# Early expert tiles: products up on two pairs of PSUM banks, and the next tile's transposes ahead of a tile's product down

## The chip, the cores and the metric

The kernel runs on one core of a Trainium2 chip. The metric is the device time of one execution in microseconds (us). The core has a tensor engine (PE, with its weight loads shown as PEld), a vector engine (DVE), a scalar engine (ACT), GpSimd (POOL) and a sync engine (SP), which here issues nearly all DMAs and does no arithmetic. Everything is in 32-bit floats. A matmul writes into PSUM; the program holds PSUM as eight banks of 128 partitions by 512 floats, and other engines read the results from there.

## The reference

The input x has shape (2, 2048, 256). Four sub-layers follow one another, each added to x, each on a layer norm of x:

```
x = x + ssm(layernorm(x))         # Mamba-2 block, 8 heads of 64, state 128, conv of 4
x = x + ffn(layernorm(x))         # mixture of experts
x = x + attention(layernorm(x))   # 16 heads of 64, softmax over the two entries of the batch
x = x + ffn(layernorm(x))         # the same mixture of experts again
```

The mixture of experts has 8 experts; a token takes the two with the highest scores:

```
idx = top_k(scores + bias, 2);  val = softmax(scores)[idx], divided by its sum
h = x @ Wl1[n] + bl1[n]                          # 256 -> 2 x 512, halves a and b
y = (silu(a) * b) @ Wl2[n] + bl2[n]              # 512 -> 256
out = sum over the token's two experts of val * y
```

The kernel computes only the products of the chosen experts. It sorts tokens by expert into tiles of up to 256 tokens.

## The kernel before

**A tile of an expert.** The class `Experts` exists twice, for the first feed-forward (`ffn`, names with `_f`) and for the last (`last`, names with `_g`). `load` (L663) issues on SP the expert's weights w1 (1 MB) and w2 (0.5 MB) and the biases b1 and b2; `rows` (L652) loads the tile's list of tokens and gates, tab; `gather` (L680) fetches the tokens' rows xs by an indirect DMA on POOL, 128 rows each. `turn` (L702) transposes xs on PE (4 matmuls against the identity, into a bank called pxs), and ACT copies the result to xT. `up_part` (L716) makes a quarter of the product up: 4 matmuls into one bank pab (the trace counts each of them as two, so 32 for a tile), then silu of the one half on ACT (sa) and the gate product on DVE (gT). `down` (L745) has 8 matmuls (16 in the trace) into a bank pf, ACT and DVE scale the result by the gate (by, y), and POOL adds y to the output in memory by two indirect DMAs.

**Early tiles.** Tokens are routed while the SSM (or, for `last`, the attention) is still going over later positions. As soon as an expert has 256 tokens from the part that is done, a tile can be computed. The dictionaries EARLY say how many such tiles there are after which group: 21 for `ffn` (names `_fe`, during the SSM), 9 for `last` (`_ge`, at the end of the attention). The rest is done by `run` (L814), where no other work stands between tiles.

The generator `early` (L790) makes the instructions of the early tiles. It yields after each half of the product up and after the product down, and the loop over the SSM's chunks (32 chunks of 128 positions, in 8 groups of 4) takes three steps of it per chunk: about one early tile per chunk. `fetch` loads two tiles ahead. Weights, xs and xT of early tiles have two buffers each, gT one.

**PSUM.** There is one pool of four tags, T, A, B and C, with two banks each, and the tags go round: the third tile of a tag waits until the first has been read. Early tiles use tag B for everything (pxs, pab, pf), and B is also used by the SSM for pb, pd and pe and by the routing. Tag A is used by the SSM for pc (the input of the conv, L990) and pz (the gate, L1037). Late tiles, in `run`, take A and B in turn for pab and T for pxs.

**The SSM's chunk.** `chunk_front` makes pz, then the decay factors lt: eight ACT instructions (L1044) on lb, which is a broadcast of the running sums over all partitions. `spread` (L1021) issues that DMA on SP two chunks ahead, into one of two buffers. Then follow exp (with a load of ACT's function table), px and pb. `chunk_back` has py, ph and pi, `chunk_out` the transposes pty and the product po.

**What sets the order.** SP's queue is in the order of the program's text; all loads stand there, and an SP instruction that waits for a buffer holds all behind it. Within a chunk SP has w1, w2, b1, b2 of the next tile and then lb. The order on PE, DVE, ACT and POOL outside `run` is set by a planner from costs and dependences, not by the text, so a change in banks can move instructions there.

Of the kernel before, what the change touches and what calls it, by code (L numbers as in the profile page):

```python
# [46 lines left out]
def kernel(  # L47
# [232 lines left out]
    class Experts:  # L280
# [509 lines left out]
        def early(self, ready):  # L790

            i = 0
            while True:
                while i >= len(self.seq):
                    yield
                if not self.seq[i][4]:
                    return
                full = sum(t[4] > 0 for t in self.seq)
                self.fetch(min(i + 2, full), min(i + 2, full))
                self.fetch(full, 0)  # L800
                if not i:
                    yield
                self.turn(i)
                t = self.ts[i]
                t["gT"] = fe.tile([P, NHT, TT], F32, tag="gT", name=f"gT_{t['nm']}", bufs=1)
                for j in range(NHT):
                    self.up_part(t, j, "B")
                    if j % 2:
                        yield
                self.down(i, "B", None)  # L810
                i += 1
                yield
# [45 lines left out]
    with tc.tile_pool(name="ssm1", bufs=1) as s1, tc.tile_pool(name="ssm2", bufs=2) as s2:  # L858
# [315 lines left out]
        for i, (b, s, t) in enumerate(chunks):  # L1174
            j = order.index((b, s)) + 1
# [365 lines left out]
```

## Time and profile before

| | us |
|---|---|
| three runs: median (lowest to highest) | 1698.82 (1694.02 to 1705.58) |
| the profiled execution | 1695.92 |
| its span | 1694.1 |

The mean granted clock of the tensor engine is 0.972 of full speed. The stages, read from the names of the instructions in the timeline, with PE's busy time in them:

| stage | window, us | PE busy, us |
|---|---|---|
| SSM, no early tiles yet | 0 to 300 | 255.3 |
| SSM with early tiles of the first feed-forward | 300 to 670 | 346.3 of 370 |
| the rest of the early tiles, alone | 670 to 740 | 63.6 of 70 |
| first feed-forward, `run` | 740 to 880 | 137.4 of 140 |
| attention | 896 to 1250 | 342.1 of 354 |
| attention's end, with the first early tiles of the last feed-forward | 1250 to 1315 | 62.5 of 65 |
| the rest of these early tiles, alone | 1315 to 1405 | 83.3 of 90 |
| last feed-forward, `run` | 1405 to 1640 | 235.0 of 235 |

In the profile's groups an arrow points from inputs to output ("pab_fe<-xT_fe,w_fe"), followed by shapes, counts, busy time in us, the mean in ns and the idle time ahead of them. In timelines and chains each row starts with its start in us and its length; brackets give the idle time before it and what ended it.

### The profile page before, as it was taken

How to read it: one execution, taken by the hardware profiler on the slowest of the kernel's cores; microseconds unless marked ns; L12 is line 12 of the kernel's file. 1: busy time of each engine (PE TensorE's matmuls, PEld its weight loads, DVE VectorE, ACT ScalarE, POOL GpSimd, SP SyncE). 2: the span in 40 equal slices, each digit the busy share in tenths (PEclk: the TensorE clock that was granted, in tenths of full speed). 3: DMA queues.
4: the chain of work that ended last, by engine and by line, in shares of the span. 5: the costliest groups of instructions: out<-in, count | busy, mean ns of one | idle time of the engine just before them, and what ended most of it. 6: DMA issues, size and time to landing. Idle time of an engine off the chain costs nothing.

```text
span 1694.1 us, 22151 instructions
## 1 busy us (share of the span) xinstructions
PE 1584.1 (94%) x7088; PEld 1193.8 (70%) x7088; DVE 897.0 (53%) x2471; ACT 670.9 (40%) x1338; POOL 736.2 (43%) x702
## 2 busy tenths in 40 slices
PE   6997988989989989999998999899999999999997
PEld 4664555677766777788885566475767878888886
DVE  6778878837648464422226757547554622222222
ACT  4886867856647543222332201101020322333322
POOL 2356357455555566634442002422240663544443
PEclk9898988999989999999999999999999999999999
DMA  4112202742535455889852231706435588888883
GB/s 157 38 54 60 88 28 61 215 126 61 168 63 160 125 144 131 209 244 320 230 133 82 54 72 52 100 13 139 144 62 150 147 215 240 222 231 229 230 215 48
DMA packets 174744, 231.30 MB, mean 137 GB/s; under 512 B 45920, under 2 KB 138080, under 8 KB 174368
## 3 DMA queue, kind: packets, MB, share of 16 engines
q1 hardware_dynamic: 143520, 193.42, 38.9%
q0 software_dynamic: 31104, 36.42, 12.0%
q8 instruction: 58, 0.95, 0.2%
q14 instruction: 62, 0.51, 0.1%
HBM read 192.72 MB, written 37.06 MB: 136 GB/s over the span
## 4 chain that ended last, share of the span: by engine, by line
PE 66%; DVE 12%; DMA 11%; POOL 5%; ACT 3%; issue 3%; SPq 1%; DVEq 0%; POOLq 0%; ACTq 0%
PE pab_g L722 9%; PE pao L1431 7%; PE pab_fe L722 5%; PE pq L1337 5%; PE pab_f L722 5%; PE pf_g L754 4%; PE pf_fe L754 4%; PE pab_ge L722 3%; DVE xc L1007 3%; PE pk L1337 3%; PE pvd L1411 3%; PE pi L1103 2%; DMA lb<-sums 2%; PE pc L990 2%; PE pf_f L754 2%
## 5 line engine op out<-in xcount | busy, mean ns | idle before, releaser
L722 PE MATMUL pab_g<-xT_g,w_g 128*128 128x256 f32 (+1 forms) x896 | 181.6, 361 | 0.0
L722 PE MATMUL pab_fe<-xT_fe,w_fe 128*128 128x256 f32 x672 | 157.8, 390 | 20.0 <-DVE gT_fe L731 17.1
L722 PEld LDWEIGHTS pab_g<-xT_g,w_g 128*128 128x128 f32 x896 | 158.5, 191 | 19.4 <-ACT xT_g L713 0.4
L722 PEld LDWEIGHTS pab_fe<-xT_fe,w_fe 128*128 128x128 f32 x672 | 128.5, 194 | 46.9 <-DVE gT_fe L731 21.8
L778 POOL DMA_INDIRECT out_dram<-y_g,tab_g x51 | 80.3, 1575 | 137.4 <-DVE y_g L767 57.9
L730 ACT ACTIVATE sa_g<-pab_g,b_g 128x256 f32<-128x256 f32 (+1 forms) x112 | 50.9, 454 | 191.3 <-PE pab_g L722 191.3
L731 DVE SCALAR_TENSOR_TENSOR gT_g<-pab_g,b_g,sa_g 128x256 f32<-128x256 f32 (+1 forms) x112 | 51.5, 460 | 129.0 <-ACT sa_g L730 129.0
L1337 PE MATMUL pq<-w_qkv_sb,axT 128*128 128x512 f32 x256 | 117.1, 597 | 0.0
L1007 DVE SCALAR_TENSOR_TENSOR xc<-pre,conv_w_sb,xc 128x512 f32<-128x512 f32 x144 | 113.3, 796 | 6.0 <-ACT xc L999 5.4
L1431 PE MATMUL pao<-w_o_sb,o 128*128 128x256 f32 x512 | 112.3, 380 | 0.0
L1431 PEld LDWEIGHTS pao<-w_o_sb,o 128*128 128x128 f32 x512 | 97.1, 190 | 15.8 <-issue 2.6
L433 POOL DMA_INDIRECT table_g<-pay_g,at_g x64 | 62.7, 980 | 86.2 <-DVE w_g L409 52.7
L990 PE MATMUL pc<-xT,w_in_sb 128*128 128x512 f32 x192 | 97.4, 638 | 0.4 <-ACT xc L999 0.4
L722 PE MATMUL pab_f<-xT_f,w_f 128*128 128x256 f32 (+1 forms) x512 | 96.6, 347 | 0.0
L754 PE MATMUL pf_g<-w_g,gT_g 128*128 128x256 f32 x408 | 92.9, 380 | 0.0
L722 PEld LDWEIGHTS pab_f<-xT_f,w_f 128*128 128x128 f32 x512 | 85.5, 191 | 9.4
L1044 ACT ACTIVATE lt<-lb,cum 128x128 f32<-128x128 f32 x256 | 82.8, 394 | 19.0 <-DMA lb<-sums 19.0
L1337 PEld LDWEIGHTS pq<-w_qkv_sb,axT 128*128 128x128 f32 x256 | 48.6, 192 | 58.8 <-issue 57.4
L1352 ACT ACTIVATE kd<-pk 128x512 f32<-128x512 f32 x32 | 19.1, 597 | 162.4 <-PE pk L1337 96.0
L778 POOL DMA_INDIRECT resid<-y_fe,tab_fe x42 | 67.0, 1595 | 37.5 <-DVE y_fe L767 21.9
L731 DVE SCALAR_TENSOR_TENSOR gT_fe<-pab_fe,b_fe,sa_fe 128x256 f32<-128x256 f32 x84 | 39.7, 480 | 80.5 <-ACT sa_fe L730 80.4
L754 PE MATMUL pf_fe<-w_fe,gT_fe 128*128 128x256 f32 x336 | 80.3, 392 | 2.2 <-DVE gT_fe L731 2.2
(477 smaller groups left out, 3368.6 us busy)
## 6 DMA issues: line engine op xcount, KB each, us to landing
w_g<-in_wl_dram SPq DMA_DIRECT2D x28, 1024.0 KB
w_fe<-in_wl_dram SPq DMA_DIRECT2D x21, 1024.0 KB
lb<-sums SPq DMA_DIRECT2D x32, 512.0 KB
w_f<-in_wl_dram SPq DMA_DIRECT2D x16, 1024.0 KB
o<-prob SPq DMA_DIRECT2D x32, 512.0 KB
w_g<-in_wl_dram SPq DMA_DIRECT2D x28, 512.0 KB
w_fe<-in_wl_dram SPq DMA_DIRECT2D x21, 512.0 KB
w_ge<-in_wl_dram SPq DMA_DIRECT2D x9, 1024.0 KB
```

The source lines that it names most:

```text
L433: i = nc.gpsimd.indirect_dma_start(out=self.table, out_offset=bass.IndirectOffsetOnAxis(ap=at[:, t, c : c + 1], axis=0), in_=pay[:, t, c, ...
L722: nc.tensor.matmul(p[:, q * n : (q + 1) * n], t["w1"][:, k, c * P : (c + 1) * P], t["xT"][:, k, :], start=(k == 0), stop=(k == KD - 1),)
L730: nc.scalar.activation(sa[:, :n], p[:, 0:n], AF.Silu, bias=t["b1"][:, i : i + 1])
L731: nc.vector.scalar_tensor_tensor(t["gT"][:, i, :n], p[:, n : 2 * n], t["b1"][:, NHT + i : NHT + i + 1], sa[:, :n], ALU.add, ALU.mult)
L754: nc.tensor.matmul(pos[h][:, h * DM : (h + 1) * DM], t["gT"][:, j, h * P : (h + 1) * P], t["w2"][:, j, :], start=(j == 0), stop=(j == NHT ...
L778: j = nc.gpsimd.indirect_dma_start(out=self.acc if self.direct else self.acc[: self.seq[i][4] or NT + TT, :], out_offset=bass.IndirectOffs ...
L990: nc.tensor.matmul(pc, w_in_sb[:, k, DI + c * P : DI + (c + 1) * P], xT[:, k, :], start=(k == 0), stop=(k == KD - 1),)
L1007: nc.vector.scalar_tensor_tensor(xc[:, c, :], pre[:, c, j : j + TG], conv_w_sb[:, c, j : j + 1], xc[:, c, :], ALU.mult, ALU.add,)
L1044: nc.scalar.activation(lt[:, i, :], lb[:, i, :], AF.Relu, bias=g["cum"][:, t, i : i + 1], scale=-1.0)
L1337: nc.tensor.matmul(p, src[:, k, t * P : (t + 1) * P], w_qkv_sb[:, k, j, half * TG : (half + 1) * TG], start=(k == 0), stop=(k == KD - 1),)
L1411: nc.tensor.matmul(pvd, w_qkv_sb[:, k, 2, c * P : (c + 1) * P], xd[:, k, :], start=(k == 0), stop=(k == KD - 1),)
L1431: nc.tensor.matmul(po[:, j * DM : (j + 1) * DM], o[i][:, c, (t + j) * P : (t + j + 1) * P], w_o_sb[:, c, :], start=(c == 0), stop=(c == NA ...
```

## The change

In `early`, three things:

```diff
                 if not i:
                     yield
-                self.turn(i)
+                if "xT" not in self.ts[i]:
+                    self.turn(i)
                 t = self.ts[i]
                 t["gT"] = fe.tile([P, NHT, TT], F32, tag="gT", name=f"gT_{t['nm']}", bufs=1)
                 for j in range(NHT):
-                    self.up_part(t, j, "B")
+                    self.up_part(t, j, "AB"[j % 2])
                     if j % 2:
                         yield
+
+                if i + 1 in self.ts and self.seq[i + 1][4]:
+                    self.turn(i + 1)
                 self.down(i, "B", None)
```

The four quarters of an early tile's product up take tags A and B in turn, where all took B. Before a tile's product down, the next tile is turned (its transposes and the copy to xT) if it has been loaded and is an early one. A tile that has been turned in this way is not turned again. The transposes of early tiles still go to tag B.

## The prediction

> **What bounds the kernel now.** I read the page's busy totals and costliest groups first, then the waits of the tensor engine (PE), then the chain of waits inside the stretch where most of them fall, then the engines' timelines there.
>
> ```profile
> PE 1584.1 (94%) x7088; PEld 1193.8 (70%) x7088; DVE 897.0 (53%) x2471; ACT 670.9 (40%) x1338; POOL 736.2 (43%) x702
> ...
> L722 PE MATMUL pab_fe<-xT_fe,w_fe 128*128 128x256 f32 x672 | 157.8, 390 | 20.0 <-DVE gT_fe L731 17.1
> ```
>
> PE is the bound: 94% of the 1694.1 us span, so all its idle time is 110 us and no removal of waits can give more. An early tile's product up (pab_fe) costs 390 ns a matmul, that of the last stage (pab_g) 361 in the same page, and 17.1 us of idle stand before it.
>
> ```profile
> PE pab_fe L722 <- DVE gT_fe L731: 17.1, 13, 4.3
> ...
> PE pab_ge L722 <- ACT xT_ge L713: 3.1, 4, 1.1
> ...
> PE pab_fe L722 <- ACT xT_fe L713: 2.7, 4, 0.7
> PE pab_ge L722 <- DVE y_ge L767: 2.5, 1, 2.5
> ```
>
> Columns: total, times, longest. The first is the wait for a PSUM bank: a pab bank is free when its gate product gT has read it. The xT rows are waits for the copy behind a tile's transposes. Why the bank is late in the stage of the SSM with early tiles (300 to 670 us) is in the chain of waits there (start, length):
>
> ```profile
> 351.17 5.87 DMA lb<-sums
> ...
> 357.37 0.97 ACT lt L1044 x3
> 358.34 0.37 ACT sa_fe L730
> 358.73 0.49 DVE gT_fe L731
> 359.22 0.04 issue
> 359.27 3.72 PE pab_fe L722 x16
> ```
>
> and in ACT's timeline of the next chunk:
>
> ```profile
> 378.78 1.57 ACT L1044 ACTIVATE lt<-lb,cum 128x128 f32<-128x128 f32 x5 [2.89 <-DMA lb<-sums]
> 380.25 0.45 ACT L730 ACTIVATE sa_fe<-pab_fe,b_fe 128x256 f32<-128x256 f32 x1
> ```
>
> ACT is in order. The SSM's lt waits for its broadcast lb; the silu sa_1 of the tile stands behind it; gT_1 behind that; and pab_2 wants that bank. lb in turn is issued on SP behind the next weight load w2, which waits for an earlier product down (pf). So pf, SP, lb, ACT, gT, PE is a loop. PE then lies idle and afterwards runs slowly:
>
> ```profile
> 378.70:381.30 2.60, 0.06 (x2) 0.03 (x1) 0.56 (x2) 2.52 (x9) 0.00 (x0) 1.00 0.14 22
> 381.30:386.70 5.40, 5.40 (x18) 4.39 (x19) 2.99 (x5) 5.01 (x7) 2.85 (x2) 0.68 0.01 0
> ```
>
> (window, PE busy, PEld, DVE, ACT, POOL, granted clock, DMA share, GB/s.) Where early tiles run alone ("tails", 670 to 740 and 1315 to 1405 us) a tile is
>
> ```profile
> 1359.98 7.17 PE L722 MATMUL pab_ge<-xT_ge,w_ge 128*128 128x256 f32 x32 [0.67 <-ACT xT_ge L713]
> 1366.99 3.67 PE L754 MATMUL pf_ge<-w_ge,gT_ge 128*128 128x256 f32 x16
> 1370.50 0.60 PE L709 MATMUL pxs_ge<-ident,xs_ge 128*128 128x128 f32 x4
> 1371.77 7.17 PE L722 MATMUL pab_ge<-xT_ge,w_ge 128*128 128x256 f32 x32 [0.67 <-ACT xT_ge L713]
> ```
>
> 11.8 us a tile, 0.67 of it idle.
>
> **The change part by part.** No instruction, byte or DMA is added or removed: 30 tiles keep their 32 up matmuls, 4 transposes, 16 down matmuls, evictions and DMAs. SP's queue, which issues w1, w2, b1, b2, the tables and lb, keeps its order exactly, so nothing is moved past a load there. What changes is bank and order on PE, ACT, DVE and POOL; the order of the changed program shows where.
>
> *Banks.* pab_1 and pab_3 stay on B with pb, pxs and pf; pab_0 and pab_2 go to A, which the SSM uses for pz and pc. pab_2 now needs the A bank that pab_0 left, whose gT_0 is ready early, and in most chunks the planner puts sa_1 ahead of lt. So the wait before pab_2 goes. By place its 13 parts are 0.26, 1.32, 2.54, 0.25, 1.05, 1.74, 4.30, 0.31, 1.48, 1.70 and 0.98 in the mixed stage (15.9) and 0.31 and 0.85 in the tail.
>
> What is late next: pf needs gT_3, which stands behind sa_2 and sa_3, and those still stand behind lt, its exp and two table loads. From pf to pf the loop is 3.45 (pf, from the chain) + 1.8 (end of pf to start of lb: 1.6, 1.8 and 2.0 in three chunks) + 6.2 (lb: 5.9, 6.2, 6.6) + 8.3 (eight lt 2.5, sz .6, bt .25, table 1.28, exp 1.06, table 1.28, two silus .9, gT .5, as in the timeline) = 19.8 us. PE's own work in a plain chunk is 19.3 (20.62 less its stall of 1.32), and about 21.7 where the next group's transposes (.9) and dt projection (1.7) fall in. So a plain chunk comes to about 19.8 instead of 20.6 to 21.2: from pf start to pf start 20.62, 20.80, 20.94 and 21.17 before, gains .8, 1.0, 1.1 and 1.4; the chunk from 594.5 (22.16) about 1.5; sum 5.8.
>
> The two long stalls are worth more. *Row:* behind the 2.54 us stall the next 16 pab take 5.41 us against 3.72 and the following pf 5.00 against 3.67, clock 0.68, .94 and .73: with the matmuls between about 3.5 us. Behind the 4.30 us one it is 6.08 and 5.00, clock 0.60: 4.1 us. *Rule:* "TensorE: Matmul & The Clock Gate", Part 1, has the array drop to half clock after about 3.4 us without activity, counted in a free-running window. By it alone the 2.54 us stall costs no clock and its chunk gains 1.3; by the row it gains more. I take the row: chunk 366 to 393 goes from 26.5 to PE's 21.7 (4.8), chunk 470 to 499 from 28.9 to 22.3 (its lb took 8.76, which lengthens the loop by 2.5): 6.6. By the rule the sum of all would be 3.5 lower.
>
> Mixed stage so far 5.8 + 4.8 + 6.6 = 17.2. Given back: pxs_fe13 waits for its gather, whose routing table comes at a fixed time after its group, so 1.9 us gained just ahead of it are lost; and around the first early tile pc_2 to pc_5 of the next group move behind the tile, about 13 us later. They feed 12 conv steps on DVE (796 ns each on the page), for which px and pb then wait. No row shows that: 0 at one end, since the group's first chunk is still a tile away; 4 at the other (near the 4.1 us that PE's pt_m waits for one DVE step elsewhere in the waits); I take 2.5. Net 12.8.
>
> *The turn ahead.* The 4 transposes and the xT copy move ahead of pf. In a tail the copy (0.6) is hidden behind pf (3.5), and the next pab follows at once: 4 x 0.68 in the first tail, 1.10 + 3 x 0.67 in the second. With the bank waits and late gT rows there (.31, .85, .88) the first tail loses 4.8 of idle. In the second, pvd now stands behind tile ge1's products, so the 2.51 for y_ge goes, with .24, .47 and 1.25 for gates: 7.6, in all about 8.
>
> The turn is also a new wait. PE's matmuls run in program order ("TensorE: Matmul & The Clock Gate", Part 2, says that only weight loads are pulled ahead), so a transpose that waits for its gather holds a pf that is ready; this speaks against the change. In the trace gathers of early tiles land well before their turn but for three waits (1.05, 1.14, 1.61), so I price it where it shows. One transpose of the run stage's first tile (pxs_f0, pxs_g0) now stands ahead of pf of the last but one early tile. Its table is loaded behind a w2 that waits for a pf: the gather lands some 11.2 (f) and 11.9 us (g) after the end of the pf before, and is wanted 7.4 after. New stalls 3.8 and 4.5, in place of 1.6 and 1.7. By the rule of no reordering this is paid in full; if PE found other work it would be nothing. I take it in full: first tail 4.8 - 2.2 = 2.6, second 8.0 - 2.8 = 5.2.
>
> *Sum:* 12.8 + 2.6 + 5.2 = 20.6 us. The profiled execution takes 1695.9 (span 1694.1 and 1.8 around it), 2.9 under the median of the three runs, 1698.8. 1695.9 - 20.6 = 1675.3; at the median 1678.
>
> **The rivals.**
> *The wait only moves.* The loop binds with its whole length and the stall before pab_2 is found again before pf, clock loss too. For: the loop's 19.8 is above PE's 19.3, and DMA lb has 25% of the chain between 325 and 400 us. Against: sa_1 no longer stands in the loop, and only two chunks had stalls that cost clock. Then the tails alone count: 1698.8 - 7.8 = 1691.
>
> *Slower: turns hold PE.* Transposes ahead of pf wait for gathers in tile after tile, because the faster chunk asks for them sooner and POOL issues them between scatters of 1.6 us. Each such stall of 2.5 to 4.3 costs 3.5 to 4.1 of clock behind it, about 7. Three use up the 20.6; six make 42, so 1698.8 + 21 = 1720. For: the three gather waits above. Against: gathers stand ahead of the scatters on POOL in the changed order, and tables are fetched tiles ahead. The same price holds if A banks shared with pc and pz make the conv late at every group.
>
> *More.* All of the 15.9 us, the 7.6 of clock and 8 in the tails go: 1698.8 - 31 = 1668. It needs lb to land sooner than the loop lets it.
>
> **How the numbers follow.** About 1%, 17 us, is what a measurement of this kernel can tell from no change. Forecast 0.45, of it 0.08 short of 17 us; more 0.12; wait only moved 0.27; slower 0.16. Faster 0.49, same 0.35, slower 0.16. The range 1663 to 1706 takes in the first three cases and two or three stalls of the slower one.
>
> **What would show it.** Right: pab_fe <- gT_fe almost gone; a new pf_fe <- gT_fe of 3 to 8 us; pab waits on xT gone; tail tiles of 11.1 us; granted clock 0.9 and more at 381 to 398 and 486 to 504; new waits of pxs_f and pxs_g of about 4 us. Wrong: pf waits as long as the pab waits were, clock under 0.8 in the mixed stage, long waits of pxs_fe for xs_fe, or px and pb waiting for conv.

## The result and the profile after

The changed kernel took 1712.1 us in the median of 16 runs (1704.1 to 1721.1), the kernel before 1699.8 us beside it: a ratio of 1.0071 with a 95% interval of 1.0056 to 1.0087. It is slower by 12 us, where 1678 and a range of 1663 to 1706 had been forecast. The profiled execution has a span of 1710.2 us, 16.1 more than before.

The page of the changed kernel, its busy totals and the row of the product up of early tiles:

```profile
PE 1598.7 (93%) x7088; PEld 1210.3 (71%) x7088; DVE 901.8 (53%) x2471; ACT 667.5 (39%) x1334; POOL 733.5 (43%) x702
...
L722 PE MATMUL pab_fe<-xT_fe,w_fe 128*128 128x256 f32 x672 | 155.8, 385 | 3.8 <-ACT xT_fe L713 2.1
```

The wait that the change was about is gone: 3.8 us of idle before pab_fe and not 20.0. Yet PE's idle time is no smaller (1710.2 - 1598.7 = 111.5 us, before 110.0), and the same 7088 matmuls keep it busy for 14.6 us longer. Idle time has moved, and PE has run more slowly. PE's waits of the changed kernel say where to (total, times, longest, in us):

```profile
PE pi L1107 <- DVE y L1093: 7.8, 5, 2.6
PE pd L925 <- ACT xT L259: 7.0, 3, 4.0
...
PE pe L972 <- DVE da L965: 5.1, 2, 4.0
...
PE pf_fe L754 <- ACT xT_fe L713: 3.5, 2, 3.2
...
PE pab_fe L722 <- DVE gT_fe L731: 1.7, 2, 1.0
```

In the kernel before, the first three of these are smaller, there is no row of pf waiting for xT, and the last row has 17.1:

```profile
PE pi L1103 <- DVE y L1089: 4.0, 5, 1.6
...
PE pe L968 <- DVE da L961: 1.3, 2, 1.1
...
PE pd L921 <- ACT xT L259: 0.5, 1, 0.5
```

A good milestone is the start of pf of the 17th early tile (pf_fe16), where the stage of the SSM with early tiles is all but over: 688.2 us before, 703.2 after. So 15.0 of the 16.1 us are lost by then. In the windows that end there (window, PE busy, PEld, DVE, ACT, POOL, granted clock, DMA share, GB/s; the kernel before first)

```profile
285.00:688.20 403.20, 375.54 (x1738) 287.62 (x1738) 245.99 (x707) 225.35 (x443) 219.46 (x194) 0.96 0.48 131
285.00:703.20 418.20, 387.36 (x1734) 300.55 (x1734) 250.37 (x700) 221.29 (x439) 217.54 (x193) 0.92 0.46 126
```

PE is busy for 11.8 us longer and idle for 3.2 us longer (30.8 and 27.7), with a lower granted clock. So about four fifths of the loss is the same work done more slowly. From there to the attention it is 222.3 us (221.0 before), and the early tiles of the last feed-forward take 156.4 (156.9).

Two places show how the loss comes about. The first is the first early tile, in PE's timeline of the changed kernel:

```profile
304.60 0.66 PE L1132 MATMUL pty<-ident,y 128*128 128x128 f32 x4 [0.23 <-DVE x L1144]
309.23 0.41 PE L972 MATMUL pe<-da,tri 128*128 128x32 f32 x2 [3.98 <-DVE da L965]
...
313.75 6.76 PE L722 MATMUL pab_fe<-xT_fe,w_fe 128*128 128x256 f32 x16 [1.40 <-ACT xT_fe L713]
```

PE waits 3.98 us for da with nothing to do, then for the copy, and the next 16 pab take 6.76 us (3.62 where the clock is full). In the kernel before, pc_2 stood ahead of pe and pc_3 ahead of pab_0, and pe waited 0.17:

```profile
305.76 1.94 PE L990 MATMUL pc<-xT,w_in_sb 128*128 128x512 f32 x4
307.87 0.41 PE L968 MATMUL pe<-da,tri 128*128 128x32 f32 x2 [0.17 <-DVE da L961]
...
311.30 3.10 PE L990 MATMUL pc<-xT,w_in_sb 128*128 128x512 f32 x4
314.23 3.62 PE L722 MATMUL pab_fe<-xT_fe,w_fe 128*128 128x256 f32 x16
```

The second place is a chunk in which the next group begins:

```profile
388.00 1.02 PE L1100 MATMUL ph<-wx,bt 128*128 128x512 f32 x2
391.48 0.51 PE L925 MATMUL pd<-w_in_sb,xT 128*128 128x16 f32 x2 [2.46 <-ACT xT L259]
391.82 0.88 PE L709 MATMUL pxs_fe<-ident,xs_fe 128*128 128x128 f32 x3
392.50 3.01 PE L925 MATMUL pd<-w_in_sb,xT 128*128 128x16 f32 x14
395.34 3.65 PE L1107 MATMUL pi<-dtx,lt 128*128 128x64 f32 x16
398.79 0.42 PE L709 MATMUL pxs_fe<-ident,xs_fe 128*128 128x128 f32 x1
399.00 5.03 PE L754 MATMUL pf_fe<-w_fe,gT_fe 128*128 128x256 f32 x16
```

ACT's timeline shows why xT is late there:

```profile
383.34 1.57 ACT L1048 ACTIVATE lt<-lb,cum 128x128 f32<-128x128 f32 x5 [2.29 <-DMA lb<-sums]
...
390.11 0.84 ACT L730 ACTIVATE sa_fe<-pab_fe,b_fe 128x256 f32<-128x256 f32 x2
390.84 1.07 ACT L259 COPY xT<-pt_a 128x512 f32<-128x512 f32 x2
```

Between these rows stand the rest of lt, its exp and two loads of ACT's function table. It is the old chain, lb, lt, exp, silus, with another end. Where pab_2 waited 2.54 us before, pd now waits 2.46; where it waited 4.30, pd waits 4.03. Behind both stands half clock, in the windows of the changed kernel (the granted clock is the third number from the end):

```profile
391.50:399.00 7.50, 7.50 (x36) 7.50 (x37) 1.75 (x6) 1.93 (x3) 2.25 (x2) 0.51 0.02 2
499.40:513.50 14.10, 14.08 (x55) 12.32 (x56) 6.05 (x23) 3.27 (x6) 5.10 (x5) 0.59 0.00 0
```

### The profile page after: what moved, and what is told of

It reads as the page before. It is cut to its first block, busy times and chain, and to the rows that moved or that the text cites. A ratio compares the mean times of both kernels' runs of the same rounds, so it can differ in the third digit from the quotient of the medians.

```text
span 1710.2 us, 22153 instructions
## 1 busy us (share of the span) xinstructions
PE 1598.7 (93%) x7088; PEld 1210.3 (71%) x7088; DVE 901.8 (53%) x2471; ACT 667.5 (39%) x1334; POOL 733.5 (43%) x702
## 3 DMA queue, kind: packets, MB, share of 16 engines
q0 software_dynamic: 31104, 36.42, 11.8%
## 4 chain that ended last, share of the span: by engine, by line
PE 69%; DVE 11%; DMA 9%; POOL 5%; ACT 4%; issue 2%; SPq 1%; DVEq 0%; POOLq 0%; ACTq 0%
PE pab_g L722 9%; PE pao L1435 6%; PE pq L1341 6%; PE pab_fe L722 6%; PE pab_f L722 5%; PE pf_g L754 4%; PE pf_fe L754 4%; DVE xc L1011 3%; PE pk L1341 3%; PE pi L1107 3%; PE pab_ge L722 3%; DMA o<-prob 3%; PE pvd L1415 3%; PE pf_f L754 3%; PE pc L994 2%
## 5 line engine op out<-in xcount | busy, mean ns | idle before, releaser
L722 PEld LDWEIGHTS pab_g<-xT_g,w_g 128*128 128x128 f32 x896 | 158.3, 190 | 19.8 <-ACT xT_g L713 0.5
L754 PE MATMUL pf_fe<-w_fe,gT_fe 128*128 128x256 f32 x336 | 85.3, 412 | 4.8 <-ACT xT_fe L713 3.5
L1107 PEld LDWEIGHTS pi<-dtx,lt 128*128 128x128 f32 x512 | 71.2, 218 | 22.2 <-DVE y L1093 12.8
L1107 PE MATMUL pi<-dtx,lt 128*128 128x64 f32 x512 | 72.8, 301 | 11.0 <-DVE y L1093 7.8
```

Source lines behind the costliest of these rows:

```text
L722: nc.tensor.matmul(p[:, q * n : (q + 1) * n], t["w1"][:, k, c * P : (c + 1) * P], t["xT"][:, k, :], start=(k == 0), stop=(k == KD - 1),)
L754: nc.tensor.matmul(pos[h][:, h * DM : (h + 1) * DM], t["gT"][:, j, h * P : (h + 1) * P], t["w2"][:, j, :], start=(j == 0), stop=(j == NHT ...
L1107: nc.tensor.matmul(pi[:, i * HD : (i + 1) * HD], f["lt"][:, i, :], f["dtx"][:, i * HD : (i + 1) * HD], start=True, stop=True,)
```

## The experiments

All ratios are to the kernel before on the same chip in the same runs. The batches differed, on four chips: the kernel before took 1707 to 1731 us there, so times are not compared from one batch to the next. The changed kernel itself was measured on the first chip only. Profiles are used to see where a wait stands, ratios for its size; the start of a pf in the tables is that of one profiled execution (the row "before" is the first chip's; a second profile, before_again, has 344.6 and 690.5). That of first_b is the fastest of its 22 runs, 17 us under their median.

### One half of the change at a time, and two repairs

Three theories stood at first: that the wait only moves along the late ACT (1), that the turn ahead makes pf wait (2), and that sharing tag A reorders the SSM's work into DVE's way (3). Later ones are told in the expectations that they belong to.

banks_only and turn_only each keep one half of the diff. swap_ba changes one string of the changed kernel:

```diff
-                    self.up_part(t, j, "AB"[j % 2])
+                    self.up_part(t, j, "BA"[j % 2])
```

after_lb_first moves one statement in the loop over chunks, so that lb is issued ahead of the next tile's weights:

```diff
+            if i + 2 < len(chunks):
+                lbs[i + 2] = spread(*chunks[i + 2])
             tiles.step()
             this = front
-            if i + 2 < len(chunks):
-                lbs[i + 2] = spread(*chunks[i + 2])
```

> Only the tags: products up of early tiles take A and B in turn; a tile is turned just before its own product up, as before. Theory 1 (the wait only moves, because the scalar engine is late with lt behind the broadcast lb): the 17 us before pab_2 go, PE waits for ACT's xT copy ahead of pd (7 us in the changed kernel) and for y ahead of pi instead, and the time is that of the changed kernel, 1.005 to 1.01 of before. Theory 2 (the turn ahead costs, since pf then waits for the next tile's copy or the last gate): 0.985 to 0.995, faster than before. Theory 3 (sharing A moves py, ph and the conv, so that PE runs into DVE): like theory 1, but with pi waiting for y at 7 us or more and without the wait of pd.

> Only the turn ahead of the product down; products up all on B as before. Theory 1: the 17 us before pab_2 are there again and nothing new stands at pd; 0.995 to 1.003 of before. Theory 2: slower than before by most of what the changed kernel lost, 1.005 to 1.01, with waits of pf for xT or the last gate. Theory 3: as before, 0.995 to 1.003.

> The changed kernel with the tags swapped, B for pab_0 and pab_2 and A for pab_1 and pab_3, so that pf takes the bank of pab_2 and not that of pab_3. Theory 2: the 0.65 us before pf in the tails and the long waits of pf for xT go, 4 to 8 us faster than the changed kernel (1.002 to 1.005 of before). Theory 1 and theory 3: the mixed stage stays as slow as in the changed kernel, at most the tails gain 3 us; 1.005 to 1.008 of before.

> The changed kernel with the issue of lb moved on SP ahead of the next tile's weight loads. Theory 1: ACT's wait of lt for lb falls from 14.5 to under 5 us, the waits of pd for xT (7.0 us) go and with them some 20 us of half clock: 0.98 to 0.99 of before. Theory 2 and theory 3: lb was not what held PE; 1.00 to 1.01 of before, waits of pi and pf unchanged.

| | ratio to before | interval | pf_fe1 starts | pf_fe16 starts |
|---|---|---|---|---|
| before | 1 | | 345.9 | 688.2 |
| changed | 1.0071 | 1.0056 to 1.0087 | 351.5 | 703.2 |
| banks_only | 1.0010 | 0.9998 to 1.0022 | 350.8 | 690.1 |
| turn_only | 0.9989 | 0.9973 to 1.0005 | 345.0 | 679.2 |
| swap_ba | 1.0053 | 1.0037 to 1.0068 | 351.0 | 695.7 |
| after_lb_first | 1.0063 | 1.0039 to 1.0087 | 351.9 | 696.8 |

Neither half alone loses anything that can be told from nothing; together they lose 0.7% (swap_ba and after_lb_first, which hold both halves and ran beside them, 0.5 and 0.6%). No theory had said so. Theory 2 falls as the main cause: the turn ahead alone reaches pf_fe16 9 us earlier than before. Theory 1 is half right: with the banks alone, pd waits 4.9 us for xT as it said, but the time isn't that of the changed kernel. But with lb issued early, pd's wait falls from 7.0 to 0.5 us and the two chunks behind it from 27.9 and 31.0 us to 22.4 each; yet the time is 1.0063, where theory 1 had said 0.98 to 0.99. ACT's row of lt in after_lb_first:

```profile
L1048 ACT ACTIVATE lt<-lb,cum 128x128 f32<-128x128 f32 x256 | 82.4, 393 | 19.8 <-PE pi L1107 17.1
```

It no longer waits for lb, but for pi to have read an older lt buffer, so ACT is now ahead, not late. Part of the gain is given back in other chunks: 3.5 us in the chunk from pf_fe1 and 7.9 in the one from pf_fe4, where pi waits 2.48 us for y and pc 2.79 for ACT's conv. At pf_fe16 6.4 us are still left of it; where these go is not shown.

swap_ba shows a smaller loss, in its trace: its time, 1.0053, can't be told from the 1.0071 of the changed kernel. A tail tile of the changed kernel, in PE's timeline:

```profile
1376.69 7.07 PE L722 MATMUL pab_ge<-xT_ge,w_ge 128*128 128x256 f32 x32
1383.60 0.60 PE L709 MATMUL pxs_ge<-ident,xs_ge 128*128 128x128 f32 x4
1384.84 3.72 PE L754 MATMUL pf_ge<-w_ge,gT_ge 128*128 128x256 f32 x16 [0.65 <-DVE gT_ge L731]
1388.40 7.07 PE L722 MATMUL pab_ge<-xT_ge,w_ge 128*128 128x256 f32 x32
```

and one of swap_ba:

```profile
723.17 7.07 PE L722 MATMUL pab_fe<-xT_fe,w_fe 128*128 128x256 f32 x32
730.08 0.60 PE L709 MATMUL pxs_fe<-ident,xs_fe 128*128 128x128 f32 x4
730.51 3.62 PE L754 MATMUL pf_fe<-w_fe,gT_fe 128*128 128x256 f32 x16
733.97 7.07 PE L722 MATMUL pab_fe<-xT_fe,w_fe 128*128 128x256 f32 x32
```

From pab to pab it is 11.7 us in the one, 10.8 in the other (not in every tile: swap_ba's pf_ge has waits for gates of its own, 8.7 us in three places). Tag B's two banks go pab_1, pab_3, pxs, pf in the changed kernel, so pf takes the bank of pab_3 and waits for the last gate; with the letters swapped it takes that of pab_2. Where another user of the tag comes between pxs and pf, as the routing's pk does, pf gets the bank of pxs and has to wait for the next tile's copy; the waits of pf for xT, 3.23 and 1.54 us at the longest, are read as this.

### The wait of pd, and the clock behind it

before_again is the kernel before, for a profile on a second chip. pd_fill puts work that nobody reads ahead of pd; xt_dve takes the two copies off ACT (transpose_group gets a parameter copy for it); split has another choice of banks.

```diff
             pd = bank("B", f"pd_{nm}")
+            if order.index((b, s)) in (6, 7):
+                for k in range(8):
+                    nc.tensor.matmul(pd[:, DM:], ident, w_in_sb[:, k % KD, :DM], start=True, stop=True)
```

```diff
-            transpose_group(xT, xn, f"a{nm}")
+            late_group = order.index((b, s)) in (6, 7)
+            transpose_group(xT, xn, f"a{nm}", copy=nc.vector.tensor_copy if late_group else nc.scalar.copy)
```

In split, `alone` is set to True behind the loop over chunks for `ffn`, and behind the attention's loop for `last`:

```diff
-                    self.up_part(t, j, "AB"[j % 2])
+                    self.up_part(t, j, "BA"[j % 2] if self.alone else "B")
```

> The kernel before, unchanged, for a profile on the same chip as the next three. Every theory expects what its first profile showed: PE waits of some 17 us for gT_fe ahead of pab_fe, about 34 us at half clock between 285 us and the end of the first early tiles.

> The changed kernel, with eight matmuls of 128x256 whose result nobody reads put ahead of pd in the last two groups, where PE stood idle for 2.46 and 4.03 us; work is added and none removed. Theory 4 (the moved wait costs by the clock: idle time followed by the thin matmuls of pd and pi keeps PE at half clock for some 10 us, where before the dense pab followed): the granted clock stays above 0.95 from pd to the end of the next pf at both places, which took 5.1 and 5.8 us of clock in the changed kernel, and the time falls by 7 to 10 us, to 1.001 to 1.003 of before. Theory 1 (waits alone count, the clock is by the way): the added work fills idle time at best, 1.006 to 1.009 of before.

> The changed kernel, with the copies of the transposed input (xT ahead of pd) of the last two groups on the vector engine and not on ACT, where they stand behind lt, exp and two silus. Theories 1 and 4: the 6.5 us that pd waited for these two copies fall to under 2, the half clock behind them goes too, 8 to 14 us in all: 0.999 to 1.003 of before. Theory 3 (py, ph and pi moved together, so that pi waits for DVE): DVE becomes later by four copies, pi waits more; 1.006 to 1.01.

> The turn ahead everywhere, products up all on B while the SSM or the attention still runs, and on B and A in turn (pab_0 and pab_2 on B) once the early tiles run alone. Theory 4 with theory 2's bank wait: the mixed stage is that of the turn ahead alone (fe16 some 9 us earlier than before, no more half clock than before), and a tail tile takes 10.8 us and not 11.7: 0.993 to 0.997 of before. Theory 1: the lb loop gives the mixed stage no gain; only the tails gain some 6 us: 0.996 to 0.998.

| | ratio to before | interval | pf_fe16 starts |
|---|---|---|---|
| before_again | one run | | 690.5 |
| pd_fill | 1.0104 | 1.0076 to 1.0133 | 704.1 |
| xt_dve | 1.0035 | 1.0020 to 1.0051 | 690.9 |
| split | 0.9922 | 0.9892 to 0.9952 | 679.5 |

xt_dve gives back half of the loss. Its waits of pd:

```profile
PE pd L926 <- DVE xT L259: 2.4, 2, 1.9
PE pd L926 <- ACT xT L259: 0.5, 1, 0.5
```

The two pairs of chunks around these copies (pf_fe2 to pf_fe4 and pf_fe6 to pf_fe8) take 53.1 and 56.4 us, against 60.4 and 59.4 in the changed kernel. So the wait that moved to pd is a cause, of some 0.36% (0.1 to 0.6, by the two intervals).

pd_fill went wrong for theory 4, and came out slower than theory 1 had said. It did hold the clock higher, in its window and its timeline:

```profile
391.50:399.00 7.50, 6.63 (x31) 4.53 (x32) 2.95 (x9) 2.73 (x5) 2.26 (x3) 0.77 0.00 0
```

```profile
387.02 3.72 PE L925 MATMUL pd<-w_in_sb,ident 128*128 128x256 f32 x16 [0.21 <-DVE gm L1074]
392.28 2.29 PE L928 MATMUL pd<-w_in_sb,xT 128*128 128x16 f32 x16 [1.54 <-ACT xT L259]
394.40 2.06 PE L1094 MATMUL py<-h,xc 128*128 128x512 f32 x2
396.25 1.75 PE L1103 MATMUL ph<-wx,bt 128*128 128x512 f32 x2
397.84 1.90 PE L1110 MATMUL pi<-dtx,lt 128*128 128x64 f32 x16
```

pd takes 2.3 us and not 3.5, pi 1.9 and not 3.65, pf 3.6 and not 5.03. But the planner put py and ph behind pd, where before they had filled PE's waiting: 3.6 us of work that the added matmuls displaced. Nothing is gained. From 285 us to pf_fe16 PE is busy for 386.3 us, of which the added matmuls are some 7.4 (two times 3.72), and idle for 32.8, against 387.4 and 30.8 in the changed kernel. So the old work takes some 8.5 us less, an estimate from these numbers, and the filling, which doesn't lie in idle time, costs as much. The experiment changed the order too; what the clock alone is worth it doesn't isolate.

split against swap_ba is the sharpest comparison: they differ only in the banks of the mixed stage, all B against B and A in turn, and the ratio is 0.9922 against 1.0053. There the alternation costs 1.3%, some 22 us, where all of the turn and the better tails are the same in both. From 285 us to pf_fe16 the time goes as follows:

| | to pf_fe16, us | PE busy | PE idle | granted clock |
|---|---|---|---|---|
| before | 403.2 | 375.5 | 27.7 | 0.96 |
| banks_only | 405.1 | 378.6 | 26.6 | 0.95 |
| turn_only | 394.2 | 367.9 | 26.3 | 0.99 |
| split | 394.5 | 367.8 | 26.8 | 0.98 |
| swap_ba | 410.7 | 381.0 | 29.7 | 0.94 |
| changed | 418.2 | 387.4 | 30.8 | 0.92 |

PE's idle time differs by 4.5 us at most, its busy time for the same work by 19.6. What separates these kernels is how long PE runs at the low clock, much more than how long it waits.

### Order, pb's bank and lb

```diff
-            tiles.step()
             aside.step(3)
             y = chunk_back(b, s, t, groups[b, s], this)
+            tiles.step()
             tiles.step()
```

is back_first (the step of the second half of the product up goes behind chunk_back). split_pb_on_a is split with `pb = bank("A", ...)`, split_lb_first is split with the move of lb shown above, split_both has both.

> The changed kernel with the second half of a tile's product up put behind chunk_back in the text, so that in the planner's order py comes ahead of pf, and pi ahead of pd. Theory 5 (with A and B in turn the planner stacks pd, py, ph and pi at the end of the chunk, where PE waits for a late ACT and DVE; the order costs, not the banks): the waits of pd for xT and of pi for y fall from 14.8 us to under 5, and the time to 0.997 to 1.003 of before. Theory 6 (whatever the order, PE that no longer waits ahead of pab_2 waits for ACT's lt, exp and silus in the same chunk): pi waits for lt, or pf for the last gate, 10 us and more; 1.005 to 1.01.

> The kernel with the turn ahead and A and B in turn only where the early tiles run alone, and with the SSM's pb on tag A and not on B, so that pab_2 no longer waits for gm to be read from pb's bank. Theory 5: the 12.8 us before pab_fe for gm go, and no thin matmul is moved behind pab_3: 0.985 to 0.990 of before. Theory 6: the wait turns up at pi or pf; 0.991 to 0.996.

> The kernel with the turn ahead and A and B in turn only where the early tiles run alone, with the issue of lb ahead of the weight loads on SP. Theory 1 (the lb loop bounds the stage): ACT's 21 us of waiting for lb go, PE's waits for gm with them; 0.983 to 0.988 of before. Theories 5 and 6: as in the changed kernel, lb earlier gives nothing that PE can use; 0.990 to 0.995.

> The last two together: the turn ahead, A and B in turn only where the early tiles run alone, pb on tag A, lb ahead of the weight loads on SP. Theory 5 (what counts is where the planner then puts pz, pb, py, ph and pi): its order puts py, ph and pi behind pab_3 again, as in the changed kernel, so the gains do not add: 0.988 to 0.995 of before. Theory 1 (the lb loop and pb's bank are separate waits of the same stage): the gains add, 0.978 to 0.985.

| | ratio to before | interval | pf_fe16 starts |
|---|---|---|---|
| back_first | 1.0099 | 1.0070 to 1.0128 | 707.8 |
| split_pb_on_a | 0.9878 | 0.9849 to 0.9907 | 673.4 |
| split_lb_first | 0.9892 | 0.9863 to 0.9921 | 678.2 |
| split_both | 0.9859 | 0.9833 to 0.9886 | 671.6 |

back_first doesn't decide: pi's and pd's waits fell from 14.8 to 9.6 us, but transposes now stood too early and waited for gathers.

```profile
PE pxs_fe L709 <- DMA xs_fe<-xnd_f,tab_fe: 15.8, 8, 3.6
```

That is the price that the prediction's slower rival named, seen here and not in the changed kernel. split_pb_on_a refutes theory 6: no pab_2 waits for gm, and a pab waits for a gate only once, 2.0 us, and PE gains. In split there is

```profile
PE pab_fe L723 <- DVE gm L1072: 12.8, 11, 2.9
```

A PE that doesn't wait before pab_2 isn't slow by itself. split_both puts py, ph and pi behind pab_3, as the changed kernel does, and is among the best; so that stacking, theory 5, isn't what costs either. Whether the gains of pb and lb add can't be told: the intervals of split_pb_on_a and split_both overlap, and those of split and split_lb_first. They ran in different batches, too. In split's profile PE waits 8.9 us in the first tail tile for something that the profile doesn't show; in those of the other three that wait is absent (0.7 us).

### The first early tile, and the sum

```diff
-                    self.up_part(t, j, "AB"[j % 2])
+                    self.up_part(t, j, "AB"[j % 2] if i else "B")
```

is first_b. first_b_dve and first_b_lb have "BA" in that place, and the copies on DVE or lb ahead of the weights.

> The changed kernel with the first early tile of each feed-forward all on B, the others on A and B in turn. Theory 7 (part of the loss is the first tile: its pab on A push the next group's pc_2 to pc_5 behind it, so that PE waits for da with nothing between): pe waits under 1 us for da and not 3.98, the first 16 pab take 3.7 us and not 6.8, and pf of the second tile starts 5 to 8 us earlier than in the changed kernel (351.5 us); the time falls to 1.001 to 1.004 of before. Against it (the lost time turns up again in the next group, whose conv was late anyway): 1.006 to 1.008.

> As first_b, with the xT copies of the last two groups on the vector engine, and B ahead of A for the other tiles, so that pf takes the bank of pab_2. Theory 7 with theory 1's waits of pd and theory 2's bank of pf: three separate losses, which add up to what the change lost; all three away gives 0.990 to 0.997 of before. Against it: they hide one another, 1.000 to 1.005.

> As first_b, with lb ahead of the weight loads on SP, and B ahead of A for the other tiles. Theory 7 with theory 1: 0.985 to 0.993 of before, as good as with all products up on B in the mixed stage, so that the banks on A cost nothing but by the first tile and the late ACT. Against it (A and B in turn costs in every group): 0.995 to 1.003.

| | ratio to before | interval | pf_fe1 starts |
|---|---|---|---|
| first_b | 1.0028 | 1.0010 to 1.0045 | 343.6 |
| first_b_dve | 0.9960 | 0.9943 to 0.9978 | 342.1 |
| first_b_lb | 0.9959 | 0.9937 to 0.9981 | 342.6 |

These two tiles of thirty, the first of either feed-forward, give back 0.43%, some 7 us (the two intervals leave 0.2 to 0.7). PE's timeline of first_b at the place shown above:

```profile
304.58 1.94 PE L994 MATMUL pc<-xT,w_in_sb 128*128 128x512 f32 x4
306.74 0.41 PE L972 MATMUL pe<-da,tri 128*128 128x32 f32 x2 [0.22 <-DVE da L965]
...
309.36 1.88 PE L994 MATMUL pc<-xT,w_in_sb 128*128 128x512 f32 x4
311.07 3.62 PE L722 MATMUL pab_fe<-xT_fe,w_fe 128*128 128x256 f32 x16
```

pc is back ahead of pe and of the first pab, pe waits 0.22, and the pab run at full clock. All runs with A and B in turn for that tile have pe's wait of 3.97 to 3.99 us, but back_first, whose order there is another; none with B has it.

The three repairs, taken alone, are worth 0.0043 (first_b), 0.0036 (xt_dve) and 0.0018 (swap_ba). 1.0071 less their sum is 0.9974; first_b_dve, which has all three, measured 0.9960, and the sum lies in its interval. So the three losses don't hide one another: that theory had 1.000 to 1.005. Without them the change is faster than before by 0.2 to 0.6%. That they add exactly is not shown, since each difference carries the error of two intervals and that of swap_ba lies within it.

first_b_lb missed its forecast. It was to be as good as with all products up on B (0.985 to 0.993), and 0.9959 lies in the range of the theory against it, by which A and B in turn cost in every group; split_lb_first, with all on B in the mixed stage, has 0.9892. Its mixed stage nearly fits the forecast: pf_fe16 starts at 681.7 us, in split_lb_first at 678.2. Behind it 1044.9 us follow in the one and 1012.6 in the other, on another chip. So a cost of the alternation beyond the three repairs is neither shown nor excluded.

## Why the prediction was wrong

**The wait before pab_2** went as forecast (17.1 to 1.7 us), and plain chunks gained more than the 19.8 us loop allowed: from pf to pf 20.62, 20.80, 20.94 and 21.17 became 19.59, 19.14, 18.97 and 19.06, a gain of 6.8 for a forecast 4.3.

From the forecast (20.6 us gained) to the profile (16.1 lost) it is 36.7 us. The two chunks with the long stalls make 14.9 of them, the tails 8.6, the first tile 3.2; the rest, net, lies in other chunks.

**The two long stalls** are the step that failed. The sum said "chunk 366 to 393 goes from 26.5 to PE's 21.7 (4.8), chunk 470 to 499 from 28.9 to 22.3 (...): 6.6". They became 27.9 and 31.0. What was late next was named as pf only; it was pd, whose copy xT stands behind the same silus on the same late ACT, and all of PE behind it. 11.4 us of gain were in truth a loss of 3.5. That the other end of the wait had been costed at the tile's own instructions, and not at every instruction of ACT behind lt, is the error: the trace of the kernel before has the xT copies in ACT's timeline, at the end of that very list:

```profile
386.72 0.47 ACT L730 ACTIVATE sa_fe<-pab_fe,b_fe 128x256 f32<-128x256 f32 x1 [0.35 <-PE pab_fe L722]
387.16 1.07 ACT L259 COPY xT<-pt_a 128x512 f32<-128x512 f32 x2
```

xt_dve shows it as a cause. The rival "the wait only moves" had this, but with a price of nothing and pf as the place.

**The first tile** was priced at 2.5 us of 0 to 4, for px and pb waiting for the conv. pf_fe1 came 5.7 us later, and first_b, which mends the first tile of both feed-forwards, gives back 7. The place was wrong too: the loss is pe's wait for da and the copy, with no pc left to fill it, and then the clock.

**The tails** were to gain 7.8 us and gained nothing (1.3 lost from pf_fe16 to the attention, 0.5 gained in the early tiles of the last feed-forward). The xT wait of 0.68 went, but pf's bank was overlooked: with pxs between, pf needs the last gate, and waits 0.65. I had followed the new bank sequence for pab, not for pf. swap_ba shows it. The new stalls of pxs_f and pxs_g, priced at 3.8 and 4.5 us, came to little (4.2 and 4.9 us in all for pxs_f before and after, 1.7 and 1.1 for pxs_g). The tail that was to reach them early didn't; that this is the reason is argued.

**The clock.** The row was weighed against the Trainium skill's rule of about 3.4 us without activity ("TensorE: Matmul & The Clock Gate", Part 1) and taken; the profile after agrees with the row: 2.46 us of idle are followed by a granted clock of 0.51 over 7.5 us. What the sum lacked is that stalls newly made have the low clock behind them as those removed did. Nor do 110 us of idle time bound the gain, as the prediction said: work at half clock counts as busy.

Not isolated: the chunk from pf_fe12 to pf_fe13, 4.2 us longer than before, where gains just ahead are lost (forecast with 1.9); the chunk from pf_fe8 to pf_fe9, 7.0 us longer, which isn't mended in xt_dve (31.7 us) and mostly is in first_b (25.8); and why the turn ahead and the banks, each harmless alone, lose together. In the turn alone, PE has ph, pi and py ahead of pd in the chunk where the 4.30 us stall was (the changed kernel only py and ph), and the stall is gone; that the banks on A take this from it is argued from the order, not shown.

## What to carry to other kernels

When a wait for a late engine is taken away, list everything that stands on that engine behind the late instruction, not only the buffer that was waited for: the consumer moves up and meets the next item of the same list. When buffers of a shared pool are given to a new user, follow the rotation for every user of the tag, in the first use as in the steady state: the first tile alone put the changed kernel 5.7 us behind. And separate stages in which an engine has other work from those in which it runs alone: the same alternation costs 1.3% in the one (swap_ba 1.0053, split 0.9922) and gains in the other (turn_only 0.9989, split 0.9922). The version chosen by stage is 0.8% faster than the kernel before, and 1.4% with pb and lb moved as well (split_both, 0.9859).

## What the runs showed of the hardware

The same program differs from batch to batch, and not evenly: the kernel before took 1699.8 us in the median on the first chip and 1707.1 to 1731.4 in the later batches. The chip alone doesn't explain it: 1707.1 and 1731.4 are both of chips listed as number 5, twelve minutes apart. Its second profile, span 1723.6, has pf_fe16 at nearly the same time (690.5 against 688.2), but the early tiles of the last feed-forward take 167.8 us and not 156.9, and the first tail tile waits 7.9 us (0.68 before). The profile puts this wait down to the copy xT, but the copy itself, a result on DVE and SP's next weight load were all released only at 703.8 us, by something outside the profile ("remote"):

```profile
703.83 0.59 ACT L713 COPY xT_fe<-pxs_fe 128x512 f32<-128x512 f32 x1 [12.64 <-remote]
...
704.47 9.89 PE L722 MATMUL pab_fe<-xT_fe,w_fe 128*128 128x256 f32 x32 [7.94 <-ACT xT_fe L713]
```

From 695.7 to 703.7 us the DMA engines moved 7 GB/s, so a crowded DMA isn't the reason there; the cause stays open. Ten other later runs have a wait of 4.8 to 9.3 us in the same place, and the first profiles of both kernels don't. A time of one batch is not a baseline for another.
